# Gate products as three float32r passes, with the pieces and sums spread over ScalarE, VectorE and GpSimd

## The chip, the cores and the metric

The kernel runs on one core of a Trainium2 chip. The core has TensorE (PE in the profile, its weight loads PEld), VectorE (DVE), ScalarE (ACT), GpSimd (POOL) and SyncE (SP), which work on their own instruction streams and wait for each other through semaphores. TensorE writes its results into PSUM, which has eight banks of 128 x 512 float32. The metric is the device time of one execution in microseconds (us); the median of the runs is what is compared.

## What is computed

Sixty-four graphs of 256 nodes with 256 features pass through two residual layers with a layer norm behind each. The first is three steps of a gated graph network with shared gate weights, the second is one graph attention layer.

```python
# layer 0: x = layernorm(x + ggnn(x))
A = (adj != 0).astype(x.dtype); h = x
for i in range(3):
    m = einsum('bnd,de->bne', h, weight[i])
    aggr = einsum('bst,bsd->btd', A, m)
    gi = aggr @ w_ih.T + b_ih;  gh = h @ w_hh.T + b_hh        # 256 -> 768 each
    r = sigmoid(i_r + h_r);  z = sigmoid(i_z + h_z)
    n = tanh(i_n + r * h_n)
    h = (1 - z) * n + z * h
# layer 1: x = layernorm(x + gat(x))
Wh = x @ W;  s1 = Wh @ a1;  s2 = Wh @ a2
e = leaky_relu(s1[:, :, None] + s2[:, None, :], 0.2)
attn = softmax(where(adj > 0, e, -9e15), axis=2)
x = layernorm(x + attn @ Wh)
```

## The kernel before

Two graphs are handled together, so there are 32 pairs. A pair's hidden state lies transposed (`hT`: 2 x 128 features by 512 nodes), so that a gate is a matmul with a 128x128 weight block held and 512 columns streamed.

At the start the weights are transposed on TensorE (L120, L128) and each layer's `weight[i]` is multiplied into `w_ih` (L140, `wc`), so that the aggregation can come first: it sums `h` over the neighbours, and the gates take the result `ag` through `wc`.

For each pair `pair(p)` then does the following.

- It compares the adjacency with zero, once as a float32r matrix `A` (L245) and once as a byte mask (L247), both on VectorE, asks for the next pair's `x` and `adj`, and transposes `x` (L161).
- It runs three layers. `split` cuts `h` into a float32r part `hi` (ScalarE, L181) and the rest `lo` (VectorE, L182). `aggregate` multiplies both with the 0/1 matrix `A` as float32r (L194) and copies the sums out as `ag`. `gates` runs for each of the two feature blocks `e` (a "gate step"): four products on full float32 (L204), for the hidden part of n, for r, for the input part of n, and for z, in that order, twelve 128x128 blocks in all; then sigmoid for r (L212), `(hn + bh) * r + n_p` (L215, L216), tanh (L217), sigmoid for z (L220), `hT - n` on GpSimd (L222), times `z` (L223) and plus `n` (L224) on VectorE. After the two steps `from_T` transposes `hT` back (L170): into the next `split`, or, after the last layer, into the residual sum `v` (L265) and a layer norm.
- It does the attention layer: the transposes of `y` (L161), `wh` with both score columns (L280), the scores' transposes (L290), sums (L292), the leaky step (L294), masking (L296, L297), the maximum (L299), exponentials (L302), transposes (L312), the weighted sum (L321, L325) and a second layer norm.

A layer norm has its statistics on VectorE (L232, L234), the power -0.5 on GpSimd (L235, L236), and its application on VectorE (L238).

`pair` is a generator with 15 steps, and two pairs are active at a time, half a run apart:

```python
steps = 4 + 3 * L + 2
while started < NP or active:
    if started < NP and (not active or (len(active) == 1 and active[0][1] >= steps // 2)):
```

That gives the order in which the instructions are written. When the program is built, the framework orders each engine's stream again: it keeps to the written order where work is ready and pulls later work ahead where it isn't, as far as tile buffers are free. On the chip each stream is fixed, and an instruction that waits holds up those behind it. Four PSUM banks serve the transposes and aggregations (`ps_t`), four the gate products (`ps_g`); most work tiles have two buffers, `x` three, `adj` two, `hT` four. Copies out of PSUM that go through `evacuate` alternate between ScalarE (L73) and VectorE (L75).

## Time and profile before

| what | us |
|---|---|
| median of three runs | 2670.46 |
| the three runs | 2670.56, 2670.46, 2669.83 |
| the profiled run | 2668.64 |
| its span, first to last instruction | 2666.5 |
| TensorE busy in it | 2611.9 |
| VectorE, ScalarE, GpSimd busy | 1281.4, 829.6, 356.8 |

The granted TensorE clock of the profiled run was 0.996 of full speed. The page gives busy times of each engine, then the chain of work that ended last, then groups of instructions: line, engine, operation, the tile written and the tiles read, shape, count, then the busy time, the mean duration of one in ns, and the idle time of the engine just before them with what ended it. In the timeline a line has the start, the duration until the last of its instructions ends, the engine, the line of the kernel and the count. Matmuls overlap in their pipeline, so their pace is read from the distance of their starts and not from their duration. One float32 product shows as two matmul instructions.

### The profile page before, as it was taken

What the parts mean: (1) busy time and instruction counts of PE and PEld (TensorE: products, weight loads), DVE (VectorE), ACT (ScalarE), POOL (GpSimd) and SP (SyncE); (2) the same over time, 40 slices, a digit from 0 to 9 for tenths busy, and PEclk for the clock granted to TensorE, in tenths of its full rate; (3) what the DMA queues carried; (4) which work ended last, traced back from release to release, by engine and by line L of the source; (5) the groups of instructions that cost most, each with busy time, mean ns of one, the idle gap of its engine ahead of it and who ended that gap; (6) DMA issues with size and microseconds to landing.
All of it is one profiled execution on the core that took longest, in us unless ns stands there. A gap on an engine that the chain in (4) does not pass through costs nothing.

```text
span 2666.5 us, 23882 instructions
## 1 busy us (share of the span) xinstructions
PE 2611.9 (98%) x8928; PEld 1441.2 (54%) x8928; DVE 1281.4 (48%) x2639; ACT 829.6 (31%) x1485; POOL 356.8 (13%) x362
## 2 busy tenths in 40 slices
PE   7999999999999999999999999999999999999996
PEld 4555555555555555555555555555555555555554
DVE  2354454545445454454554545454454544545544
ACT  2233332333323333232333323333233332333332
POOL 1111111111111111111111111111111111111111
PEclk9999999999999999999999999999999999999998
DMA  3000000000000000000000000000000000000000
GB/s 95 9 16 24 16 24 16 24 16 19 22 16 24 16 24 16 16 24 18 23 24 16 24 16 24 16 16 24 16 24 16 24 16 16 24 16 16 8 0 16
DMA packets 53522, 54.48 MB, mean 20 GB/s; under 512 B 1696, under 2 KB 53408, under 8 KB 53408
## 3 DMA queue, kind: packets, MB, share of 16 engines
q1 hardware_dynamic: 52256, 51.91, 6.1%
q8 instruction: 70, 1.15, 0.2%
q10 hardware_dynamic: 1056, 1.05, 0.1%
q14 instruction: 44, 0.36, 0.0%
q0 software_dynamic: 96, 0.01, 0.0%
HBM read 36.18 MB, written 16.78 MB: 20 GB/s over the span
## 4 chain that ended last, share of the span: by engine, by line
PE 92%; DVE 4%; ACT 1%; POOL 1%; issue 1%; DMA 0%; SPq 0%; POOLq 0%; DVEq 0%; ACTq 0%
PE pg L204 73%; PE pa L194 7%; PE pwh L280 4%; PE pt L170 3%; PE po L321 2%; PE pt L161 2%; PE pt L312 1%; DVE v L325 1%; ACT z L220 1%; DVE st_b L232 1%; PE pw L140 1%; DVE o L238 1%; POOL rs_b L236 1%; PE s L290 1%; DVE d L223 1%
## 5 line engine op out<-in xcount | busy, mean ns | idle before, releaser
L204 PE MATMUL pg<-ag,wc 128*128 128x512 f32 x2304 | 1051.4, 592 | 0.0
L204 PEld LDWEIGHTS pg<-ag,wc 128*128 128x128 f32 x2304 | 437.9, 190 | 550.8 <-issue 542.2
L204 PE MATMUL pg<-hT,whhT 128*128 128x512 f32 x1536 | 719.5, 592 | 0.0
L204 PEld LDWEIGHTS pg<-hT,whhT 128*128 128x128 f32 x1536 | 276.4, 190 | 261.5 <-issue 260.6
L223 DVE TENSOR_TENSOR d<-d,z 128x512 f32<-128x512 f32 x192 | 132.8, 692 | 526.7 <-ACT z L220 500.5
L212 ACT ACTIVATE r<-pg,b_sum 128x512 f32<-128x512 f32 x192 | 131.9, 687 | 785.6 <-PE pg L204 785.4
L215 DVE SCALAR_TENSOR_TENSOR n<-pg,bh,r 128x512 f32<-128x512 f32 x192 | 144.0, 750 | 443.6 <-ACT r L212 443.6
L204 PE MATMUL pg<-xT,whhT 128*128 128x512 f32 x768 | 350.6, 592 | 0.0
L222 POOL TENSOR_TENSOR d<-hT,n 128x512 f32<-128x512 f32 x128 | 161.8, 1264 | 968.3 <-ACT n L217 968.3
L217 ACT ACTIVATE n<-n,bi 128x512 f32<-128x512 f32 x192 | 138.3, 720 | 300.7 <-DVE n L216 298.9
L220 ACT ACTIVATE z<-pg,b_sum 128x512 f32<-128x512 f32 x192 | 131.9, 687 | 315.6 <-PE pg L204 313.6
L204 PEld LDWEIGHTS pg<-xT,whhT 128*128 128x128 f32 x768 | 141.2, 190 | 153.5 <-issue 145.4
L222 POOL TENSOR_TENSOR d<-xT,n 128x512 f32<-128x512 f32 x64 | 80.9, 1264 | 513.6 <-ACT n L217 513.6
L216 DVE TENSOR_TENSOR n<-n,pg 128x512 f32<-128x512 f32 x192 | 132.1, 688 | 32.3 <-PE pg L204 25.5
L194 PE MATMUL pa<-A,lo_h 128*128 128x256 f32 x512 | 131.9, 299 | 12.2 <-DVE lo_h L182 12.1
L194 PE MATMUL pa<-A,hi_h 128*128 128x256 f32 x512 | 139.7, 309 | 0.0
L224 DVE TENSOR_TENSOR hT<-d,n 128x512 f32<-128x512 f32 x192 | 132.3, 689 | 5.5
L280 PE MATMUL pwh<-gw,yT 128*128 128x258 f32 x512 | 125.9, 388 | 0.6 <-ACT yT L73 0.5
L321 PE MATMUL po<-wh,eT 128*128 128x256 f32 x512 | 119.1, 381 | 0.0
L194 PEld LDWEIGHTS pa<-A,lo_h 128*128 128x128 f32 x512 | 95.8, 190 | 39.5 <-DVE lo_h L182 38.6
L280 PEld LDWEIGHTS pwh<-gw,yT 128*128 128x128 f32 x512 | 95.8, 192 | 38.2 <-issue 14.6
L170 PE MATMUL pt<-ident,hT 128*128 128x128 f32 x768 | 108.7, 274 | 2.9 <-DVE hT L224 2.9
(90 smaller groups left out, 2188.7 us busy)
## 6 DMA issues: line engine op xcount, KB each, us to landing
x<-in_x_dram SPq DMA_DIRECT2D x32, 512.0 KB, 3.8
adj<-in_adj_dram SPq DMA_DIRECT2D x32, 512.0 KB, 3.8
out_dram<-o SPq DMA_DIRECT2D x32, 512.0 KB, 2.9
w_n<-in_L_gnn_weight_dram ACTq DMA_DIRECT2D x1, 768.0 KB, 9.4
wi_n<-in_L_gnn_w_ih_dram SPq DMA_DIRECT2D x1, 768.0 KB, 7.0
wh_n<-in_L_gnn_w_hh_dram SPq DMA_DIRECT2D x1, 768.0 KB, 11.2
gw<-in_L_gnn_W_dram ACTq DMA_DIRECT2D x1, 256.0 KB, 10.4
bi<-in_L_gnn_b_ih_dram POOLq DMA_DIRECT2D x1, 3.0 KB, 8.0
```

What stands on the lines that cost most here:

```text
L170: nc.tensor.transpose(pt[:, (c * C + d) * P:(c * C + d + 1) * P], hT[:, d, (g * C + c) * P:(g * C + c + 1) * P], ident)
L194: nc.tensor.matmul(pt[:, g * N:(g + 1) * N], t[:, g, s, d * P:(d + 1) * P], A[:, g, s, :], start=(n == 0), stop=(n == len(todo) - 1))
L204: nc.tensor.matmul(pt, w[:, d, o * P:(o + 1) * P], m[:, d, :], start=(n == 0), stop=(n == len(todo) - 1))
L215: nc.vector.scalar_tensor_tensor(n, hn, bh[:, 2 * C + e:2 * C + e + 1], r, op0=ALU.add, op1=ALU.mult)
L216: nc.vector.tensor_add(n, n, n_p)
L217: nc.scalar.activation(n, n, AF.Tanh, bias=bi[:, 2 * C + e:2 * C + e + 1])
L220: nc.scalar.activation(z, z_p, AF.Sigmoid, bias=b_sum[:, C + e:C + e + 1])
L222: nc.gpsimd.tensor_sub(d, hT[:, e, :], n)
L223: nc.vector.tensor_mul(d, d, z)
L224: nc.vector.tensor_add(hT_new[:, e, :], d, n)
L280: nc.tensor.matmul(pt[:, :D + 2], yT[:, d, k * P:(k + 1) * P], gw[:, d, :], start=(d == 0), stop=(d == C - 1))
L321: nc.tensor.matmul(pt[:, c * D:(c + 1) * D], eT[:, g, j, c * P:(c + 1) * P], wh[:, g, j, :], start=(j == 0), stop=(j == C - 1))
```

## The change

The gate weights and both inputs of the gate products (`ag` and the hidden state) are kept as three float32r pieces each: H, the upper 12 bits; L, the rest; and D = H - L / U with U = 2^-12 (for the weights L is held scaled by 1 / U, and D is H - L). A gate product becomes two PSUM sums: the first of H x H and L x L, the second of D x D, and the result is `(1 + U) * first - U * second`. A gate step thus has 36 float32r matmuls of 512 columns in eight sums where it had 24 float32 instructions in four, and the order of the four products is now r, hidden n, z, input n.

ScalarE reads each first sum out of PSUM with the factor; VectorE subtracts the second sum from PSUM; the sigmoids then read SBUF. `r * hn`, the sum before tanh, `hT - n` and the product with `z` run on GpSimd, and the last add on VectorE; `hT` is updated in place. The pieces of `ag` are made by ScalarE (H), VectorE (L) and VectorE (D); those of the hidden state by ScalarE, GpSimd and VectorE. The adjacency comparisons and the lower half of `x` move to GpSimd, the application of the layer norm to ScalarE. In the attention layer the leaky step becomes part of the ScalarE operation (Prelu), and the mask is written over the scores in place.

PSUM is divided three to five banks; `x` has two buffers, `adj` one, `hi` and `lo` one, `hT` two, and the tiles of the attention layer one (`y` two). The core of the diff, cut:

```diff
-    io = ctx.enter_context(tc.tile_pool(name="io", bufs=3))
+    io = ctx.enter_context(tc.tile_pool(name="io", bufs=2))
-    ps_t = ctx.enter_context(tc.tile_pool(name="ps_t", bufs=4, space=bass.MemoryType.PSUM))
-    ps_g = ctx.enter_context(tc.tile_pool(name="ps_g", bufs=4, space=bass.MemoryType.PSUM))
+    ps_t = ctx.enter_context(tc.tile_pool(name="ps_t", bufs=3, space=bass.MemoryType.PSUM))
+    ps_g = ctx.enter_context(tc.tile_pool(name="ps_g", bufs=5, space=bass.MemoryType.PSUM))
...
+    def upper(dst, src):
+        nc.scalar.activation(dst, src, AF.Copy, scale=1.0 - 2.0 ** -13)
+    def lower(eng, dst, src, hi):
+        eng.tensor_sub(dst, src, hi.bitcast(F32))
+    def cross(dst, hi, lo):
+        nc.vector.scalar_tensor_tensor(dst, lo.bitcast(F32), -1.0 / U, hi.bitcast(F32),
+                                       op0=ALU.mult, op1=ALU.add)
+    def cut_weight(dst, src, tmp):
+        upper(dst[0], src)
+        lower(nc.vector, tmp, src, dst[0])
+        nc.vector.tensor_scalar(dst[1], tmp, 1.0 / U, None, op0=ALU.mult)
+        nc.vector.tensor_sub(dst[2], dst[0].bitcast(F32), dst[1].bitcast(F32))
...
+    def cut_T(hT, name):
+        cut = pieces(work, [P, C, GN], name, "h")
+        upper(flat(cut[0]), flat(hT))
+        lower(nc.gpsimd, flat(cut[1]), flat(hT), flat(cut[0]))
+        cross(flat(cut[2]), flat(cut[0]), flat(cut[1]))
+        return cut
...
-            evacuate(ag[:, d, :], pt)
+            upper(ag[0][:, d, :], pt)
+            lower(nc.vector, ag[1][:, d, :], pt, ag[0][:, d, :])
+        cross(flat(ag[2]), flat(ag[0]), flat(ag[1]))
...
-        hid, inp = (whhT, hT), (wc[:, i], ag)
-        hn = product(2 * C + e, [hid])
-        r_p = product(e, [hid, inp])
-        nc.scalar.activation(r, r_p, AF.Sigmoid, bias=b_sum[:, e:e + 1])
-        n_p = product(2 * C + e, [inp])
-        nc.vector.scalar_tensor_tensor(n, hn, bh[:, 2 * C + e:2 * C + e + 1], r, op0=ALU.add, op1=ALU.mult)
-        nc.vector.tensor_add(n, n, n_p)
+            for kinds in ((0, 1), (2,)):
+                pt = ps_g.tile([P, GN], F32, tag="g", name=f"pg_{name}_{o}")
+                todo = [(w[k], m[k], d) for k in kinds for w, m in parts for d in range(C)]
...
+        def less(dst, b, rest):
+            nc.vector.scalar_tensor_tensor(dst, b, -U, rest, op0=ALU.mult, op1=ALU.add)
+        hid, inp = (whh, hc), (wc[i], ag)
+        a, b = product(e, [hid, inp])
+        nc.scalar.activation(r, a, AF.Copy, scale=1.0 + U)
+        less(r, b, r)
+        nc.scalar.activation(r, r, AF.Sigmoid, bias=b_sum[:, e:e + 1])
+        a, b = product(2 * C + e, [hid])
+        nc.scalar.activation(n, a, AF.Identity, scale=1.0 + U, bias=bh[:, 2 * C + e:2 * C + e + 1])
+        less(n, b, n)
+        nc.gpsimd.tensor_mul(n, n, r)
+        a, b = product(C + e, [hid, inp])
+        nc.scalar.activation(z, a, AF.Copy, scale=1.0 + U)
+        less(z, b, z)
+        nc.scalar.activation(z, z, AF.Sigmoid, bias=b_sum[:, C + e:C + e + 1])
+        a, b = product(2 * C + e, [inp])
+        nc.scalar.activation(t, a, AF.Copy, scale=1.0 + U)
+        less(t, b, t)
+        nc.gpsimd.tensor_add(n, n, t)
         nc.scalar.activation(n, n, AF.Tanh, bias=bi[:, 2 * C + e:2 * C + e + 1])
-        z_p = product(C + e, [hid, inp])
-        nc.scalar.activation(z, z_p, AF.Sigmoid, bias=b_sum[:, C + e:C + e + 1])
+        d = temp("t")
         nc.gpsimd.tensor_sub(d, hT[:, e, :], n)
-        nc.vector.tensor_mul(d, d, z)
-        nc.vector.tensor_add(hT_new[:, e, :], d, n)
+        nc.gpsimd.tensor_mul(d, d, z)
+        nc.vector.tensor_add(hT[:, e, :], d, n)
...
-            nc.vector.tensor_scalar(dst[:, k // C, k % C, :], v[:, k // C, k % C, :],
-                                    mv[:, k, 0:1], rs[:, k:k + 1], op0=ALU.subtract, op1=ALU.mult)
+            nc.scalar.activation(dst[:, k // C, k % C, :], v[:, k // C, k % C, :], AF.Identity,
+                                 scale=rs[:, k:k + 1], bias=nm[:, k:k + 1])
...
-        nc.vector.tensor_scalar(A, a_sb, 0.0, None, op0=ALU.not_equal)
+        nc.gpsimd.tensor_scalar(A, a_sb, 0.0, 0.0, op0=ALU.is_equal, op1=ALU.is_equal)
-        nc.vector.tensor_scalar(mask, a_sb.rearrange("p g c n -> p (g c) n"), 0.0, None, op0=ALU.is_gt)
+        nc.gpsimd.tensor_scalar(mask, a_sb.rearrange("p g c n -> p (g c) n"), 0.0, None, op0=ALU.is_le)
...
-        hi, lo, _ = split([(g, x_sb[:, g].rearrange("p c d -> p (c d)")) for g in range(G)], f"x_{p}")
+        nc.scalar.copy(whole[1], whole[0])
+        lower(nc.gpsimd, whole[2], whole[0], whole[1])
+        hc = cut_T(hT, f"x_{p}")
...
-                                 bias=s1[:, k:k + 1])
-        nc.vector.scalar_tensor_tensor(sc, sc, ALPHA, sc, op0=ALU.mult, op1=ALU.max)
-        nc.gpsimd.memset(em, NEG_INF)
-        nc.vector.copy_predicated(em, mask, sc)
+            nc.scalar.activation(sc[:, k, :], s2r[:, (k // C) * N:(k // C + 1) * N], AF.Prelu,
+                                 bias=s1[:, k:k + 1], alpha=ALPHA)
+        nc.vector.copy_predicated(sc.rearrange("p k n -> p (k n)"), mask.rearrange("p k n -> p (k n)"),
+                                  neg.to_broadcast([P, K * N]))
```

## The prediction

> **What bounds the kernel now.** I read the page's busy shares first, then the chain that ended last, then the groups.
>
> ```profile
> PE 2611.9 (98%) x8928; PEld 1441.2 (54%) x8928; DVE 1281.4 (48%) x2639; ACT 829.6 (31%) x1485; POOL 356.8 (13%) x362
> ...
> PE 92%; DVE 4%; ACT 1%; POOL 1%; issue 1%; DMA 0%; SPq 0%; POOLq 0%; DVEq 0%; ACTq 0%
> ...
> L222 POOL TENSOR_TENSOR d<-hT,n 128x512 f32<-128x512 f32 x128 | 161.8, 1264 | 968.3 <-ACT n L217 968.3
> L217 ACT ACTIVATE n<-n,bi 128x512 f32<-128x512 f32 x192 | 138.3, 720 | 300.7 <-DVE n L216 298.9
> ```
>
> TensorE is the bound and the other engines have room; the chain's line list puts 73% of the span on the gate matmuls (L204). A 128x512 operation costs 1.264 us on GpSimd and about 0.7 us on the others. The windows view gives the steady period, two pairs long, and the drain at the end; the timeline shows how the same product runs in both.
>
> ```profile
> 1310.92:1473.05 162.13, 161.10 (x553) 88.78 (x553) 79.54 (x166) 51.37 (x92) 22.09 (x22) 1.00 0.06 20
> ...
> 2630.00:2666.50 36.50, 15.12 (x58) 11.47 (x56) 16.51 (x46) 6.84 (x17) 2.52 (x4) 0.70 0.04 14
> ```
>
> ```profile
> 1355.24 3.65 PE L280 MATMUL pwh<-gw,yT 128*128 128x258 f32 x16
> ```
>
> ```profile
> 2637.60 5.52 PE pwh L280 x16
> ```
>
> The columns after the length are busy times of PE, PEld, DVE, ACT, POOL, then the granted clock. One pair takes 162.13 / 2 = 81.07 us; 32 pairs are 2594 us, so 72 us of the 2666.5 us span are start and drain. In the drain, where PE stands idle for about 5 us at a time (2630.3 to 2635.2), the clock falls to 0.70 and `pwh` takes 5.52 us for 3.65. Last, the timeline at the boundary between two GRU layers:
>
> ```profile
> 1383.49 3.62 PE L321 MATMUL po<-wh,eT 128*128 128x256 f32 x16
> ...
> 1383.69 0.69 ACT L220 ACTIVATE z<-pg,b_sum 128x512 f32<-128x512 f32 x1 [1.93 <-PE pg L204]
> 1384.48 0.69 DVE L223 TENSOR_TENSOR d<-d,z 128x512 f32<-128x512 f32 x1 [3.53 <-ACT z L220]
> 1385.20 0.69 DVE L224 TENSOR_TENSOR hT<-d,n 128x512 f32<-128x512 f32 x1
> ...
> 1386.94 1.04 PE L170 MATMUL pt<-ident,hT 128*128 128x128 f32 x8
> ...
> 1390.53 1.38 DVE L238 TENSOR_SCALAR o<-v,mv_b,rs_b 128x256 f32<-128x256 f32 x4 [0.90 <-POOL rs_b L236]
> ...
> 1391.83 0.69 DVE L182 TENSOR_TENSOR lo_h<-pt,hi_h 128x512 fp32r<-128x512 f32 x1
> ...
> 1394.23 0.59 PE L204 MATMUL pg<-ag,wc 128*128 128x512 f32 x1
> ```
>
> From the last gate product (1383.49) to the next layer's first product on the new `ag` (1394.23) are 10.74 us, and PE idles only 0.8 us of it: it does the other pair's `po`, the transposes, the aggregation, and hidden-state products pulled ahead. This cover is what the change uses up. The view also shows blocking: the second `lo_h` waits behind `o`, which waits for GpSimd.
>
> **The products.** A gate step has 12 weight blocks. Now each is two f32 instructions: eight of them start at 1322.77 and the next at 1326.20, so 0.429 us each, 24 x 0.429 = 10.29 us. Then it is 36 float32r instructions of 512 columns, a form that the trace lacks. Bounds: half an f32 instruction, if that is two passes, 0.2145 us; or twice the 256-column float32r step of L194 (16 starts from 1308.97 about 0.119 us apart), 0.237 us. So 7.72 to 8.55 us. I take the lower, of the same width; the upper keeps a cost per weight load that is paid once, not twice, at 512 columns. Six steps a pair save 6 x 2.57 = 15.4 us (upper end 10.4). The PE floor is 81.07 - 15.4 = 65.7 us per pair.
>
> **The other engines**, over the whole run. DVE loses L215, L216, L223, half the `ag` copies, `lo_x`, both adjacency comparisons, the layer-norm applications and the leaky step (144 + 132 + 133 + 65 + 41 + 44 + 88 + 39 = 686 us), and gains 768 combinations from PSUM at 0.750 (L215), 192 subtractions at 0.66 (L182) and 192 full-width combinations at 1.226 (L294): 576 + 127 + 235 = 938. So 1281 + 252 = 1533, 48 us per pair. ACT gains 768 PSUM reads at 0.587 to 0.687 (the `ag` copy, the sigmoid), 96 more for `ag`, 96 upper halves of 1024 elements at about 1.1, 256 layer-norm applications at 0.49 (L302): some 490 + 66 + 106 + 125, so 1617, 51 us per pair. GpSimd gains 576 gate operations at 1.264, 128 subtractions of 1024 elements at about 2.5, and two adjacency comparisons a pair (nearest rows: the 1024-element fill at 0.953, twice L222 at 2.53), and loses the fill: 357 + 728 + 320 + 110 - 30 = 1485, 46 us per pair. None reaches 65.7: PE remains the bound on load alone.
>
> **The gate's tail.** After the last product came sigmoid, multiply, add: 2.4 us to 1385.89. Now there follow the subtraction of the second sum (0.75), a GpSimd add (1.264), tanh (0.72), GpSimd subtract and multiply (2 x 1.264), DVE add (0.69): 5.95 us, six hand-overs at 0.08 us (tanh's end to L222's start), and about 0.3 us until ScalarE has read the first sum, whose last matmul ends 0.43 us earlier. That is 6.7 us, 4.3 more. Between two steps of a layer this is hidden, since the next step's products need nothing of it. At a layer boundary it is not: 10.74 + 4.3 = 15.0 us, or 16.1 if the hidden state's upper half (1.1) stands on ScalarE ahead of `hi`. The lower half and the difference piece run beside the transposes and the aggregation, so I take nothing for them (0.6 us if late). PE has in it of this pair the transposes 0.87, the aggregation 16 x 0.119 = 1.9, and at most 16 hidden products at 0.2145 = 3.4 (five PSUM banks): 6.2 us. There remain 8.8 to 9.9 us. The other pair's attention and input transposes are 0.87 + 3.5 + 0.4 + 0.87 + 3.45 + 0.87 = 10 us a pair, 5 for each of the two inner boundaries (the third lies under the next pair's layer 0). So 3.8 to 4.9 us stay open, 7.6 to 9.8 us a pair, unless the next pair's first layer is pulled in; the trace shows pulls (its `pa` at 1331.11 lies ahead of the older pair's remaining L170). Between 0 and 9.8 I take 6: pulled work needs a free `x` buffer, and the blocking at 1391.83 says that queues add to it. A period of 71.7 us.
>
> **Waits.** ScalarE's tanh now waits for GpSimd, and so do its layer-norm applications (for `rs`); behind them stand the other pair's PSUM reads. DVE's `hT` add waits for GpSimd too; behind it stand the other pair's combinations and `lower`. Five banks of eight sums let PE run about 5 us ahead, which covers such a wait (the first rival is where it doesn't). With two `x` buffers the load of p+1 waits on the SP queue for pair p-1's residual add, and with one `adj` buffer for pair p's GpSimd comparisons; outputs can stand behind it. Landing takes 3.8 us, most of a pair's time lies between, DMA share is 0.06: nothing, or 3.8 us a pair if that cover is gone. The leaner softmax (no leaky step, no fill) shortens a chain that lies beside the other pair's products: nothing. Whether Prelu costs a third table load (1.283 us, now two a pair) no row shows; ACT has room.
>
> **Start and drain.** Cutting the weights puts three DVE operations and one ACT operation where 16 copies were; the matmuls wait on them: 10 to 20 us, I take 15. The last pair has no cover for three tails: 13 us.
>
> Sum: 32 x 71.7 + 72 + 28 = 2394 us span; the profiled run had 2.1 us around it (2668.64) and lies 1.8 us under the median: about 2398, and I say 2395.
>
> **A shared port.** No GpSimd subtraction overlaps a DVE operation with two SBUF inputs in this trace, which therefore can't show what overlap does. [...] By rows alone: the DVE side is 6 adds at 0.69, 6 combinations at 1.226 and the predicated copy at 1.305, 12.8 us a pair; free overlap costs nothing, and full exclusion makes 46 + 12.8 = 59 us, still under 65.7, but can put one more 1.264 us on each of two hand-overs per boundary: 5 us a pair, 2555 us. I keep zero in the sum and this end in the range.
>
> **Rivals.** (1) Slower: in-order queues bind the gate step. If each step's combinations stand behind the previous step's `hT` add, and evacuations behind sigmoid and tanh, the step is a ring: 4 x 0.75 + 3 x 0.72 + 2 x 0.69 + 3 x 1.264 + 0.69 = 11.0 us with 13 hand-overs at 0.08, 12.1 us, against 10.29 now. Six of them and twice the 8.3 us that now lie between `hT` and the `ag` products are 89 us: 32 x 89 + 104 = 2952 us. It decides once the period passes (2666 - 100) / 32 = 80.2 us, that is with half of the steps bound so. For it: the wait at 1390.53. Against: hidden products are pulled ahead of blocked work, and in the timeline most gate steps stand beside attention work, not beside another pair's gate step. (2) All gaps filled: 65.7 us, 32 x 65.7 + 104 = 2206 us. (3) The products at 0.237 us, or the port in full: 76.7 us, 2558 us. (4) Nothing pulled ahead, and the gaps cool the clock: the drain's 5 us gap made `pwh` and the transposes some 2.5 us longer; 65.7 + 9.8 + 5 = 80.5 us, 2680 us, no gain.
>
> **How the numbers follow.** Forecast 0.50, rival 2 0.15, rival 3 0.15, rival 4 0.07, rival 1 0.13. Over 0.2% (5 us, about what can be told from no change) faster: 0.83; within: 0.02; slower: 0.15. The range reaches from rival 2 past rival 3 and leaves out rivals 4 and 1, 0.20: 2200 to 2640.
>
> **What would show it.** Right: gate matmuls 0.215 us apart, a two-pair period near 143 us, PE idle some 3 us ahead of each inner aggregation, its matmuls waiting on `hi` or `lo`, and a clock of 1.00. Wrong: starts 0.237 us apart; PE waiting within a gate step on ACT or DVE for a free bank; a clock under 0.95 in the steady part; `hT` waiting long on `d` with GpSimd idle.

## The result, and the profile after

The changed kernel takes 3245.6 us (median of four, 3244.0 to 3246.5) against 2670.5 us before: 1.215 times as long, 95% interval 1.213 to 1.218. The forecast was 2395 us and faster. First the page's busy shares, utilisation of TensorE over 40 slices, and granted clock (9 is 90% or more):

```profile
PE 2666.3 (82%) x11232; PEld 2082.6 (64%) x11232; DVE 1598.8 (49%) x2807; ACT 1540.2 (48%) x2677; POOL 1594.9 (49%) x1099
...
PE   6878888888888888878888888888888888888886
...
PEclk9988888898888888888889898888889888888887
```

The three helper engines carry about what the prediction gave them (50, 48 and 50 us a pair; forecast 48, 51, 46). None is near its limit, and yet TensorE, 98% busy before, is at 82%, and many of its slices are at a clock under 0.9. So load isn't the answer; waiting is. The windows view over two pairs gives the period, 198.2 / 2 = 99 us a pair (81 before, 71.7 forecast), with the clock at 0.86:

```profile
1303.00:1501.20 198.20, 165.41 (x698) 129.59 (x697) 98.50 (x173) 95.70 (x168) 99.66 (x69) 0.86 0.05 17
```

The groups that the gate step's chain runs through (busy time, mean ns of one, then the idle time ahead of them and what ended it):

```profile
L268 POOL TENSOR_TENSOR n<-n,r 128x512 f32<-128x512 f32 x192 | 246.9, 1286 | 674.5 <-ACT r L264 573.6
L281 DVE TENSOR_TENSOR hT<-t,n 128x512 f32<-128x512 f32 x192 | 227.2, 1184 | 465.9 <-POOL t L280 465.9
...
L277 ACT ACTIVATE n<-n,bi 128x512 f32<-128x512 f32 x192 | 138.4, 721 | 231.2 <-POOL n L276 231.2
```

GpSimd stands 674 us at the multiplication by `r`; while it stands, everything behind it in its queue stands too. VectorE stands 466 us at the `hT` addition for GpSimd, and the addition itself takes 1.184 us on average, for 0.69 before. TensorE's own waits, by what ended them (us in total, times, longest; `aD` is the piece D of `ag`, `lo_h` the rest of the next layer's `h`):

```profile
PE pt L209 <- DVE hT L281: 193.3, 64, 7.2
PE pg L248 <- DVE aD L97: 81.0, 32, 4.0
PE pt L379 <- ACT sc L369: 42.5, 33, 6.3
PE pg L248 <- DVE r L257: 32.6, 16, 2.1
PE pa L233 <- DVE lo_h L94: 28.0, 15, 2.0
```

Three places in the timeline show how these waits come about.

**The tail at a layer boundary**, which the prediction drew for the old kernel between 1383.49 and 1394.23:

```profile
1681.12 1.76 DVE L281 TENSOR_TENSOR hT<-t,n 128x512 f32<-128x512 f32 x1 [1.48 <-POOL t L280]
1681.75 3.62 PE L388 MATMUL po<-wh,eT 128*128 128x256 f32 x16
...
1682.80 0.68 DVE L257 SCALAR_TENSOR_TENSOR z<-pg,z 128x512 f32<-128x512 f32 x1
1683.51 0.72 ACT L272 ACTIVATE z<-z,b_sum 128x512 f32<-128x512 f32 x1 [3.30 <-DVE z L257]
1684.14 0.58 ACT L274 ACTIVATE t<-pg 128x512 f32<-128x512 f32 x1
1684.75 0.69 DVE L257 SCALAR_TENSOR_TENSOR t<-pg,t 128x512 f32<-128x512 f32 x1 [1.27 <-ACT t L274]
...
1685.59 1.27 POOL L276 TENSOR_TENSOR n<-n,t 128x512 f32<-128x512 f32 x1 [3.26 <-DVE t L257]
...
1690.33 0.69 DVE L281 TENSOR_TENSOR hT<-t,n 128x512 f32<-128x512 f32 x1 [2.86 <-POOL t L280]
...
1691.07 1.54 PE L209 MATMUL pt<-ident,hT 128*128 128x128 f32 x6 [4.46 <-DVE hT L281]
...
1696.74 0.39 PE L233 MATMUL pa<-A,lo_h 128*128 128x256 f32 x1 [1.87 <-DVE lo_h L94]
...
1699.79 0.63 PE L248 MATMUL pg<-aH,wc2H_wc 128*128 128x512 f32 x1
```

The last gate product ends where `po` begins, 1681.75; `hT` is done at 1691.02. That is 9.3 us, 2.6 more than the forecast 6.7: the combination of `z` stood behind the previous block's `hT` addition (1681.12, stretched to 1.76), the reading of the next sum behind z's sigmoid, and so on. The whole boundary is 18.0 us (10.74 before, 15.0 to 16.1 forecast), TensorE idles 0.8 + 4.46 + 1.87 = 7.1 us of it, and the clock is half for 6.6 us of the time from 1691 to 1701.

**A tiny operation that blocks two queues:**

```profile
1594.05 3.72 POOL L304 TENSOR_SCALAR A<-adj 128x1024 fp32r<-128x1024 int32 x1 [1.05 <-PE pa L233]
...
1597.74 2.37 POOL L94 TENSOR_TENSOR lo_x<-x,hi_x 128x1024 fp32r<-128x1024 f32 x1
...
1601.46 0.16 DVE L295 SCALAR_TENSOR_TENSOR nmr_b<-mv_b,rs_b 128x4 f32<-128x4 f32 x1 [4.44 <-POOL rs_b L293]
1601.54 1.22 DVE L97 SCALAR_TENSOR_TENSOR aD<-aL,aH 128x1024 fp32r<-128x1024 f32 x1
1601.66 2.07 ACT L297 ACTIVATE y<-y,nmr_b,rs_b 128x256 f32<-128x256 f32 x4 [4.96 <-DVE nmr_b L295]
...
1602.82 1.22 PE L248 MATMUL pg<-aD,wc2D_wc 128*128 128x512 f32 x2 [4.04 <-DVE aD L97]
```

`aL` was ready at 1597.0. But on VectorE the 0.16 us `nmr_b` of the other pair's layer norm stood ahead of `aD`, waiting for `rs_b`, which on GpSimd lay behind the adjacency comparison and `lo_x`. TensorE lost 4.04 us to a chain that has nothing to do with the product. Then, in two windows, before and after this gap (busy PE, PEld, DVE, ACT, POOL, and the clock):

```profile
1594.40:1598.40 4.00, 4.00 (x18) 3.09 (x18) 2.62 (x8) 1.71 (x3) 4.00 (x2) 1.00 0.01 4
...
1603.00:1608.50 5.50, 5.50 (x13) 4.33 (x14) 1.74 (x3) 2.71 (x6) 1.27 (x1) 0.50 0.29 97
```

At a clock of 0.50 the matmuls follow each other at 0.427 us instead of 0.234: the gap was paid for twice.

**An addition beside a GpSimd subtraction:**

```profile
1515.85 2.38 POOL L94 TENSOR_TENSOR hL_x<-hT,hH_x 128x1024 fp32r<-128x1024 f32 x1
1515.92 2.85 DVE L281 TENSOR_TENSOR hT<-t,n 128x512 f32<-128x512 f32 x1 [4.37 <-POOL t L280]
1518.70 0.68 DVE L257 SCALAR_TENSOR_TENSOR r<-pg,r 128x512 f32<-128x512 f32 x1
...
1519.42 0.74 PE L248 MATMUL pg<-aH,wc2H_wc 128*128 128x512 f32 x2 [2.03 <-DVE r L257]
```

The addition of 0.69 us lasts 2.85, from just behind the start of GpSimd's subtraction to 0.5 us after its end; the combination behind it is late, and TensorE waits 2.03 us for the bank. Of the 192 `hT` additions of the run 61 are stretched like this: 31 beside this subtraction (2.83 us on average), 15 beside the multiplication by `r` (1.76) and 15 beside the mask's comparison (1.52); the median is 0.693.

**A ledger of TensorE's time.** I give each shape of matmul its 20th percentile of start-to-start times as its pace at full clock, and multiply by its count (work); add up the idle times in front of TensorE's instructions (idle); and call what remains of the stretch from its first to its last instruction the rest. Before: work 2584, idle 46, rest 20 us. After: 2206, 566, 447. The rest holds what the half clock cost, but not only that. Half of the time that TensorE was busy while the granted clock was 0.50 is an estimate of that cost: 344 us after, 4 before. What remains, about 100 and 16 us, lies at full clock, in starts further apart than the 20th percentile; why, no run says. The texts written before the runs call the whole rest half clock, which is too much. The passes did save 377 us of TensorE's work. Idle time took back 520, and the rest 427, of it 340 by the half clock.

### The profile page after: what moved, and what is told of

Its sections match the earlier page's. It is cut to its first block, busy times and chain, and to the rows that moved or that the text cites. A ratio compares the mean times of both kernels' runs of the same rounds, so it can differ in the third digit from the quotient of the medians.

```text
span 3241.9 us, 31208 instructions
## 1 busy us (share of the span) xinstructions
PE 2666.3 (82%) x11232; PEld 2082.6 (64%) x11232; DVE 1598.8 (49%) x2807; ACT 1540.2 (48%) x2677; POOL 1594.9 (49%) x1099
## 3 DMA queue, kind: packets, MB, share of 16 engines
q10 hardware_dynamic: 1056, 1.05, 0.1%
## 5 line engine op out<-in xcount | busy, mean ns | idle before, releaser
L268 POOL TENSOR_TENSOR n<-n,r 128x512 f32<-128x512 f32 x192 | 246.9, 1286 | 674.5 <-ACT r L264 573.6
L281 DVE TENSOR_TENSOR hT<-t,n 128x512 f32<-128x512 f32 x192 | 227.2, 1184 | 465.9 <-POOL t L280 465.9
L276 POOL TENSOR_TENSOR n<-n,t 128x512 f32<-128x512 f32 x192 | 246.3, 1283 | 423.6 <-DVE t L257 422.5
L209 PE MATMUL pt<-ident,hT 128*128 128x128 f32 x768 | 180.7, 363 | 248.5 <-DVE hT L281 193.3
L279 POOL TENSOR_TENSOR t<-hT,n 128x512 f32<-128x512 f32 x192 | 246.2, 1282 | 163.7 <-ACT n L277 163.7
L248 PE MATMUL pg<-hH_h,whhH_whh 128*128 128x512 f32 x768 | 292.4, 457 | 0.0
L248 PE MATMUL pg<-hD_h,whhD_whh 128*128 128x512 f32 x768 | 265.0, 424 | 2.8 <-DVE hD_h L97 1.0
L248 PE MATMUL pg<-hL_h,whhL_whh 128*128 128x512 f32 x768 | 257.1, 406 | 0.0
L280 POOL TENSOR_TENSOR t<-t,z 128x512 f32<-128x512 f32 x192 | 246.2, 1282 | 15.1
L94 POOL TENSOR_TENSOR hL_h<-hT,hH_h 128x1024 fp32r<-128x1024 f32 x64 | 151.9, 2373 | 125.3 <-ACT hH_h L91 125.3
L349 PE MATMUL pwh<-gw,yT 128*128 128x258 f32 x512 | 166.0, 464 | 25.1 <-ACT wh L79 20.1
L248 PEld LDWEIGHTS pg<-hD_h,whhD_whh 128*128 128x128 f32 x768 | 150.0, 199 | 39.6 <-DVE hD_h L97 8.0
```

The lines of the kernel that those rows point to most:

```text
L94: eng.tensor_sub(dst, src, hi.bitcast(F32))
L209: nc.tensor.transpose(pt[:, (c * C + d) * P:(c * C + d + 1) * P], hT[:, d, (g * C + c) * P:(g * C + c + 1) * P], ident)
L248: nc.tensor.matmul(pt, w[:, d, o * P:(o + 1) * P], m[:, d, :], start=(n == 0), stop=(n == len(todo) - 1))
L268: nc.gpsimd.tensor_mul(n, n, r)
L276: nc.gpsimd.tensor_add(n, n, t)
L279: nc.gpsimd.tensor_sub(d, hT[:, e, :], n)
```

## The experiments

Three theories stood at first. (1) Late chains: the gate's tail and what hangs on it make TensorE wait, and the waits cool the clock. (2) The denser float32r passes pull the clock down by themselves. (3) GpSimd's and VectorE's new loads, and a port that I took the two to share (an addition of 0.69 us lasts 2.85 beside a GpSimd subtraction at 1515.92; the port itself no run shows). For each run the table gives the time, the ratio to the kernel before, and the ledger, with the estimate of what the half clock cost; the order is by time.

| kernel | us | ratio, 95% interval | work | idle | rest | of it half clock |
|---|---|---|---|---|---|---|
| no_pool | 2387.1 | 0.8945 [0.893, 0.896] | 2210 | 91 | 60 | 5 |
| room | 2397.6 | 0.8978 [0.8965, 0.8992] | 2211 | 97 | 66 | 9 |
| put_back | 2407.5 | 0.9017 [0.9002, 0.9032] | 2198 | 101 | 84 | 7 |
| one_sum | 2476.6 | 0.9276 [0.926, 0.9291] | 2209 | 146 | 103 | 36 |
| order_only | 2506.2 | 0.939 [0.9363, 0.9417] | 2192 | 163 | 127 | 13 |
| after_one_sum | 2514.2 | 0.9416 [0.9389, 0.9444] | 2199 | 176 | 115 | 28 |
| (before) | 2670 | 1 | 2584 | 46 | 20 | 4 |
| ring_vec | 2705.6 | 1.0136 [1.0116, 1.0156] | 2203 | 290 | 187 | 96 |
| ring_only | 2711.6 | 1.0158 [1.0138, 1.0179] | 2192 | 296 | 199 | 84 |
| two_sums_vec | 2762.1 | 1.0349 [1.0319, 1.0379] | 2210 | 314 | 212 | 73 |
| ring_pool | 2875.5 | 1.077 [1.0748, 1.0791] | 2203 | 380 | 269 | 166 |
| low_dve | 3034.7 | 1.1366 [1.1333, 1.1399] | 2206 | 447 | 356 | 243 |
| mid_dve | 3053.8 | 1.1437 [1.1404, 1.147] | 2210 | 468 | 353 | 236 |
| cut_chain | 3077.3 | 1.1525 [1.1502, 1.1548] | 2206 | 548 | 302 | 192 |
| two_sums_hl | 3078.6 | 1.1531 [1.1507, 1.1554] | 2207 | 502 | 348 | 246 |
| z_last | 3136.8 | 1.1748 [1.1725, 1.1772] | 2200 | 518 | 396 | 259 |
| adj_dve | 3170.6 | 1.1875 [1.1851, 1.1899] | 2207 | 580 | 359 | 229 |
| (after) | 3245.6 | 1.2154 [1.2133, 1.2175] | 2206 | 566 | 447 | 344 |
| warm | 3294.9 | 1.234 [1.2305, 1.2376] | 2371 | 526 | 371 | 274 |

### one_sum: the passes alone

The kernel before, with only its products cut into passes; tiles share buffers to make room.

```diff
-            todo = [(w, m, d) for w, m in parts for d in range(C)]
+            todo = [(w[j], m[k], d) for j, k in ((0, 0), (0, 1), (1, 0)) for w, m in parts for d in range(C)]
...
+    def cut(dst, src):
+        nc.scalar.activation(dst[0], src, AF.Copy, scale=1.0 - 2.0 ** -13)
+        nc.vector.tensor_sub(dst[1], src, dst[0].bitcast(F32))
```

> The kernel before with its gate products alone made three float32r passes, all into one PSUM sum (H x H, H x L, L x H; the term L x L is left out); the pieces come from ScalarE and VectorE, the gate's tail, the adjacency and the layer norm stay as they were. Theory 1 (late chains, then a cooled clock): the tail stays 2.4 us, so the cover of the boundaries holds; 36 x 0.234 = 8.4 us a step against 10.29 saves 11 us a pair, period near 70 us, about 2350 us, clock over 0.97. Theory 2 (dense float32r passes pull the granted clock down by themselves): clock near 0.87, no faster than 2600 us.

2476.6 us at a clock of 0.982, with 11232 matmuls as in the changed kernel and TensorE at 94%. Theory 2 falls: as many passes, more densely packed, keep the clock. Theory 1's 2350 us isn't reached either; 127 us are missing, with 146 us of idle time. The passes by themselves take 7% off the kernel before; with what came along, the changed kernel takes 1.31 times as long as this one (3245.6 / 2476.6).

### cut_chain, adj_dve, z_last: one suspect at a time

Cut_chain leaves the recurrence out: inner layers go on from the old state, so that nothing waits for the tail, and the result isn't the network's; adj_dve has both comparisons on VectorE; z_last takes the input-n products ahead of z's.

```diff
-        nc.vector.tensor_add(hT[:, e, :], d, n)
+        nc.vector.tensor_add(hT[:, e, :] if i == L - 1 else d, d, n)
```

> The changed kernel, but in the first two layers the new state is written into a scratch tile and the next layer goes on from the old state: the recurrence over layers is left out, every instruction is still there. Theory 1: the transposes, pieces and aggregation of the next layer no longer wait for the tail; most of the 566 us of PE's idle time and of the 447 us at half clock go; 2350 to 2550 us, clock over 0.95. Theory 2 (the clock follows the float32r work): clock stays near 0.87, over 2900 us. Theory 3 (GpSimd's and VectorE's loads and the port they share): the loads are unchanged, over 2900 us.

```diff
-        nc.gpsimd.tensor_scalar(A, a_sb, 0.0, 0.0, op0=ALU.is_equal, op1=ALU.is_equal)
+        nc.vector.tensor_scalar(A, a_sb, 0.0, None, op0=ALU.not_equal)
...
-        nc.gpsimd.tensor_scalar(mask, a_sb.rearrange(...), 0.0, None, op0=ALU.is_le)
+        nc.vector.tensor_scalar(mask, a_sb.rearrange(...), 0.0, None, op0=ALU.is_le)
```

> The changed kernel with both adjacency comparisons back on VectorE (0.69 us each there; 3.66 and 2.78 us on GpSimd in the changed kernel's trace). Theory 1: only waits behind these two go, as the 4.0 us at 1602.8 on the piece aD; with the clock 100 to 250 us, so 3000 to 3150 us. Theory 3 (GpSimd's long operations are the main cause): below 2900 us.

```diff
+        a, b = product(2 * C + e, [inp])    # with its reads, addition, tanh and subtraction
         a, b = product(C + e, [hid, inp])   # with its reads and sigmoid
-        a, b = product(2 * C + e, [inp])
```

> The changed kernel with the order of the last two products of a gate step exchanged: input n before z, as in the kernel before. Theory 1: behind the last product stand then evacuation, combination, sigmoid, GpSimd multiply and add instead of combination, add, tanh, subtract, multiply, add; 2 to 3 us less on each of two inner boundaries, and with the clock 150 to 350 us less: 2900 to 3100 us. Theories 2 and 3: loads and products are the same, so within 30 us of 3246 us.

They gain 168, 75 and 109 us, and TensorE's idle time hardly moves (548, 580, 518 for 566). All three miss the range that theory 1 gave them; adj_dve and z_last miss those of the other theories too, while cut_chain's time is what theory 3 gave (over 2900 us). In adj_dve one wait did go as expected: the longest for `aD` is 1.7 us, where behind `nmr_b` it had been 4.0. In cut_chain the wait for `hT` at the boundary is all but gone (7.9 us, once), and others have grown or come in its place:

```profile
PE pg L248 <- ACT aH L91: 99.4, 46, 3.9
PE pwh L349 <- ACT wh L79: 75.2, 31, 3.2
...
PE pg L248 <- DVE hD_x L97: 58.1, 16, 3.9
```

In the changed kernel these were 19.2, 20.1 and 0.3 us. So taking away the tail at the boundary doesn't take away the idle time. I read it so that the in-order queues are late as a whole, and whichever product comes next meets it: the first theory in a wider form than the one I had written. This is argued, not shown. The framework also orders each kernel's streams anew (VectorE's stand in another order in cut_chain than in the changed kernel), and no run separates that from the waits.

### after_one_sum: the gate section put back

```diff
-            for kinds in ((0, 1), (2,)):
-                pt = ps_g.tile(...)          # two sums, pieces H, L, D
+            pt = ps_g.tile(...)              # one sum: HH, HL, LH
...
-        nc.gpsimd.tensor_mul(n, n, r)        # and ScalarE's reads, the combinations
+        nc.vector.scalar_tensor_tensor(n, hn, bh[...], r, op0=ALU.add, op1=ALU.mult)
```

> The changed kernel with the gate section alone put back: the three passes of a gate go into one PSUM sum, and the elementwise work of a gate step is that of before (ScalarE reads two sums, VectorE combines, GpSimd only subtracts); pieces are upper and lower alone, the third pass leaves the smallest product out. The adjacency comparisons and lower halves stay on GpSimd, the layer-norm application on ScalarE, the leaner attention part too. Two-sum theory (the combinations and the ring through GpSimd in each gate step make TensorE's inputs late): 2450 to 2560 us, TensorE idle under 200 us, clock over 0.97. Spread theory (GpSimd's long comparisons and lower halves, and the layer-norm constants behind them, hold the in-order queues; the gate section is innocent): still over 2900 us, idle over 400 us. Both in part: between 2600 and 2850 us.

2514.2 us, clock 0.987: in the range of the two-sum theory. 731 of the 838 us that separate the changed kernel from put_back (further down) go with the gate section: its sums, its pieces, and its ring, that is the chain of small operations from the reading of a sum to the new `hT`. The comparisons and lower pieces on GpSimd and the layer norm on ScalarE are all still there.

### mid_dve, low_dve, warm: parts of it, and the clock

```diff
-        nc.gpsimd.tensor_mul(n, n, r)
+        nc.vector.tensor_mul(n, n, r)
...
-        nc.gpsimd.tensor_add(n, n, t)
+        nc.vector.tensor_add(n, n, t)
```

> The changed kernel with two of the four GpSimd operations of a gate step (the multiplication by r and the addition of the input product) on VectorE; 12 of 24 a pair, 8.3 us more of VectorE's time a pair for 15.2 us less of GpSimd's. Queue theory (GpSimd stands at the multiplication until r is there, 574 us in all, and holds back the row constants, lower halves and subtractions behind it): GpSimd's wait for r is gone, VectorE's wait for the layer-norm constants falls from 143 us to under 80, 2950 to 3150 us. Load theory (what counts is how much VectorE carries; it goes from 50 to 58 us a pair): no gain, 3220 to 3300 us.

```diff
-        lower(nc.gpsimd, flat(cut[1]), flat(hT), flat(cut[0]))
+        lower(nc.vector, flat(cut[1]), flat(hT), flat(cut[0]))
...
-        lower(nc.gpsimd, whole[2], whole[0], whole[1])
+        lower(nc.vector, whole[2], whole[0], whole[1])
```

> The changed kernel with the lower pieces of the hidden state and of x (128 subtractions of 1024 elements) on VectorE instead of GpSimd. Shared-port theory (a GpSimd subtraction of 2.4 us that starts with the VectorE addition of hT stretches it from 0.69 to 2.85 us): the mean of the hT addition falls from 1.18 us to under 0.80, VectorE's wait for hL vanishes, 3000 to 3150 us. If neither the port nor the length of that operation is on the path that sets the end: 3200 to 3280 us, with the mean of hT down all the same.

```diff
             pt = bank("pt")
+            for n in range(warm if g == 0 else 0):      # 24 at inner boundaries
+                nc.tensor.transpose(pt[:, n % 4 * P:(n % 4 + 1) * P], ident, ident)
```

> The changed kernel with 24 transposes of the identity put ahead of the transposes at each inner layer boundary, written to the bank that those overwrite: 64 x 24 at 0.11 us, 166 us more TensorE work, standing where TensorE waits for hT (193 us in all). Clock theory (it is the gap that sets the clock to half for some us after it): idle down by 120 us or more, half-clock loss down from 447 us to under 350, and the time no longer than 3245 us although there is more to do. If the clock doesn't follow these gaps, or other gaps open in their place: half-clock loss 400 us or more, and 3270 to 3410 us.

Mid_dve gains 192 us although VectorE carries more, as the queue theory had it. One of its steps missed: VectorE's wait for the layer-norm constants didn't fall under 80 us, it stayed at 141 (112.6 and 28.1). The gain shows elsewhere: TensorE's wait for `hT` falls from 193.3 to 98.7 us, and none of the `hT` additions is stretched any more (0.692 us on average), although the lower pieces are still GpSimd's. How much of the 192 us is the queue and how much the stretched additions, the run doesn't separate. Low_dve gains 211 us; the mean of the `hT` addition falls to 0.839 us, not under 0.80, since 30 additions are still stretched, 15 beside the multiplication by `r` and 15 beside the mask's comparison.

Warm settles the clock only in part. 165 us more work cost 49 us: idle fell by 40 us, not by 120, and the rest by 76, of it the half clock by 70. The time is in the second range. So filling gaps with useless work raised the clock here (0.866 to 0.900), but where TensorE had been waiting it now waits a little later.

### ring_pool and two_sums_hl: the gate section, part by part

Ring_pool is after_one_sum with the changed kernel's order of products and its elementwise ring:

```diff
-        nc.vector.scalar_tensor_tensor(n, hn, bh[...], r, op0=ALU.add, op1=ALU.mult)
-        nc.vector.tensor_add(n, n, n_p)
...
-        nc.vector.tensor_mul(d, d, z)
...
+        nc.scalar.activation(n, product(2 * C + e, [hid]), AF.Identity, bias=bh[...])
+        nc.gpsimd.tensor_mul(n, n, r)
...
+        nc.scalar.copy(t, product(2 * C + e, [inp]))     # after z's product
+        nc.gpsimd.tensor_add(n, n, t)
...
+        nc.gpsimd.tensor_mul(d, d, z)
```

> One PSUM sum for each gate product (the third pass without the smallest product, pieces upper and lower alone), but the elementwise ring of the changed kernel: ScalarE reads all four sums, and the multiplication by r, the addition, the subtraction and the multiplication by z are GpSimd's, 24 a pair. What is gone against the changed kernel: the second sums, their 768 combinations on VectorE and the difference pieces. If the ring through GpSimd makes TensorE late: over 2800 us, idle over 350 us. If the second sums and the difference pieces do: 2500 to 2620 us, idle under 230 us. In mid_dve half of the ring's way through GpSimd was worth 190 us, so about 2510 + 300 = 2810 us if the ring's share adds up.

Two_sums_hl is the changed kernel without the difference pieces:

```diff
-            for kinds in ((0, 1), (2,)):
+            for kinds in (((0, 0), (0, 1)), ((1, 0),)):
...
-        cross(flat(cut[2]), flat(cut[0]), flat(cut[1]))
```

> The changed kernel with two sums a gate, the same combinations and the same ring through GpSimd, but of upper and lower pieces alone: the first sum holds upper x upper and upper x lower, the second lower x upper (the smallest product is left out); the difference pieces, 192 combinations of 1024 elements at 1.22 us on VectorE and their place between a piece and the products, are gone. If the difference pieces are what is late (TensorE's waits for aD and hD, some 110 us, and the half clock after them): 2950 to 3050 us. If the combinations and the ring are: 3100 to 3230 us, with TensorE's waits moved to aL and hL.

With after_one_sum and the changed kernel these make a ladder, in this order: 2514 without any of it; 2876 with the ring; 3079 with the second sums and their 768 combinations as well; 3246 with the difference pieces. The ring costs 361 us, the second sums 203, the difference pieces 167. Ring_pool lies in the range of its first theory (over 2800 us, idle over 350: 380), 65 us over the third figure; two_sums_hl lies between its two ranges. Ring_pool's largest waits are those of the ring:

```profile
PE pt L207 <- DVE hT L260: 198.1, 95, 6.4
...
DVE hT L260 <- POOL t L259: 687.0, 177, 12.7
```

### ring_vec, ring_only, order_only: what makes the ring dear

```diff
-        nc.gpsimd.tensor_mul(n, n, r)                    # ring_vec, in ring_pool
+        nc.vector.tensor_mul(n, n, r)                    # and so the addition of t and the multiplication by z
```

> Ring_pool with three of its four GpSimd operations a gate step (the multiplication by r, the addition, the multiplication by z) on VectorE; the order of the products and ScalarE's four reads stay. If the engine is the cause (each of the three takes 1.28 us instead of 0.69 and keeps GpSimd's queue closed while it waits): 2500 to 2580 us. If the order of the products (the input product last, tanh behind it) is the cause: 2700 us or more. By the length of the operations alone, two of them in the tail at 64 inner boundaries, 0.6 us each: 2875 - 77 = 2798 us.

2705.6 us, in the range of the order theory: the engine of three operations is worth 170 us, twice what the length of two of them in the tail would give (77). The other 191 us remain.

```diff
-        upper(flat(cut[0]), flat(hT))                    # ring_only: ring_pool's gate step in put_back
-        lower(nc.gpsimd, flat(cut[1]), flat(hT), flat(cut[0]))
+        for d in range(C):
+            upper(cut[0][:, d, :], hT[:, d, :])
+            lower(nc.vector, cut[1][:, d, :], hT[:, d, :], cut[0][:, d, :])
```

> Put_back (2407.5 us) with the GpSimd ring of ring_pool in the gate step and nothing else on GpSimd but the row constants: the comparisons and the lower pieces stay on VectorE. If the ring is slow by its own length and hand-overs: 2650 to 2780 us, about as much over put_back as ring_pool is over after_one_sum (361 us). If it is slow only because it shares GpSimd's queue with the long comparisons and lower pieces: 2420 to 2520 us.

2711.6 us, 304 over put_back. The ring is dear even when GpSimd has little else to do; sharing its queue with comparisons and lower pieces adds the rest (ring_pool is 164 over ring_only, after_one_sum 107 over put_back: 57 us more with the ring than without).

```diff
-        hn = product(2 * C + e, [hid])                   # put_back: hn, r, n_p, z
         r_p = product(e, [hid, inp])
+        hn = product(2 * C + e, [hid])
...
         z_p = product(C + e, [hid, inp])
+        n_p = product(2 * C + e, [inp])                  # order_only: r, hn, z, n_p; its addition and tanh after it
```

> Put_back (2407.5 us) with only the order of a gate step's products that the change has: r, hidden n, z, input n, so that the addition, tanh, subtraction, multiplication and hT addition all follow the last product, where put_back has only the sigmoid of z, a multiplication and an addition there. Nothing else moves. If the order carries what the engine doesn't (ring_vec stayed 191 us over after_one_sum): 2560 to 2620 us, with TensorE waiting for hT at the 64 inner boundaries. If ScalarE's two more reads carry it: 2400 to 2450 us.

2506.2 us: the order alone costs 99 us. I expected 150 to 210 if the order carried all that ring_vec left, so it carries about half. Whether ScalarE's two more reads carry the other 92, or the order is dearer in ring_vec's surroundings, or it is the buffers (in the ring `t` and the difference `hT - n` share two, in after_one_sum the difference has two for itself), stays open. TensorE's wait for `hT` in order_only is only 17.3 us (5.4 in put_back). Its idle time rises by 62 us in several places: it waits 28.0 us for a `wh` that put_back never waits for, 18.1 for `lo_h` (8.5), 22.8 for `eT` (17.5).

### two_sums_vec: can the two sums be kept?

```diff
-        nc.gpsimd.tensor_mul(n, n, r)                    # in z_last
+        nc.vector.tensor_mul(n, n, r)                    # and so the addition of t and the multiplication by z
```

> The changed kernel, its two sums and difference pieces kept, with the input-n products ahead of z's (as in z_last) and three of the four GpSimd operations of the gate step on VectorE. If engine and order in the gate step are most of the loss, the two gains add: 3245 - 108 (z_last) - 190 to 300 (mid_dve and the third operation) = 2840 to 2950 us. If they carry it nearly whole: under 2700 us, and the two sums would pay. VectorE then carries 62 us a pair.

2762.1 us: order and engine together are worth 483 us, more than I had added up (up to 409). But it falls between the two ranges and stays 3.5% over the kernel before. Its largest wait, `pg <- aD`, 71.1 us, is not one for the difference piece's own length: all 16 of these waits stand behind `nmr_b`, which waits for GpSimd's `rs_b` as at 1601.46. GpSimd still has the comparisons and lower pieces there. Put_back has them on VectorE and is 107 us under after_one_sum; whether two sums would pay with that too, no run shows.

### put_back, room, no_pool: a faster kernel

Put_back is after_one_sum with comparisons and lower pieces on VectorE; what remains of the change is the three passes, the layer norm on ScalarE and the leaner attention part. Room adds buffers:

```diff
-    io = ctx.enter_context(tc.tile_pool(name="io", bufs=2))
+    io = ctx.enter_context(tc.tile_pool(name="io", bufs=3))
...
-    # in words: ps_t 3 banks, ps_g 5 banks; late, hi, lo and adj: 1 buffer
+    # in words: ps_t 4 banks, ps_g 4 banks; late, hi, lo and adj: 2 buffers
+    # and the hidden state's pieces are made in gates(), per feature block
```

> After_one_sum with the lower pieces, by blocks of 512, and the adjacency comparisons back on VectorE; the leaner attention part and the layer-norm application on ScalarE stay. Its waits there for hL (50 us) are gone: 2440 to 2480 us, idle under 140 us, against 2477 us for one_sum; if VectorE's larger load (36 to 44 us a pair) matters more: 2500 to 2540 us.

> Put_back with more buffers (three for x, two for adj, for the pieces of h and for the tiles of the attention part), four banks for either kind of PSUM tile instead of three and five, and the hidden state's pieces cut as soon as each feature block is done: 2420 to 2460 us and a clock over 0.985 if waits for free tiles hold the attention part; 2450 to 2480 us if they do not.

No_pool takes the last gate operation off GpSimd:

```diff
-        nc.gpsimd.tensor_sub(d, hT[:, e, :], n)
+        nc.vector.tensor_sub(d, hT[:, e, :], n)
```

> Room (2397.6 us) with the last GpSimd operation of the gate step, the subtraction h - n, on VectorE as well: the tail is 0.6 us shorter, VectorE carries 4 us a pair more. 2380 to 2395 us if the tail is still on the path at the layer boundaries (64 x 0.6 = 38 us at most), 2395 to 2405 us if it is hidden.

2407.5, 2397.6 and 2387.1 us; the last is 10.6% under the kernel before. Put_back and room are faster than I expected, no_pool is in its first range. Room's buffers, banks and earlier pieces together bring 10 us. Put_back is 69 us under one_sum, so what is left of the change (the leaner attention part, the layer norm on ScalarE, its division of buffers) does help once the gate step isn't in its way; these parts were not run one by one. The timeline at a layer boundary of no_pool, to be held against that of the changed kernel above:

```profile
1210.97 0.63 PE L242 MATMUL pg<-aH,wc0L_wc 128*128 128x512 f32 x2
1211.44 3.65 PE L334 MATMUL pwh<-gw,yT 128*128 128x258 f32 x16
1211.64 0.69 ACT L258 ACTIVATE z<-pg,b_sum 128x512 f32<-128x512 f32 x1 [1.19 <-PE pg L242]
1212.36 0.69 DVE L261 TENSOR_TENSOR d<-d,z 128x512 f32<-128x512 f32 x1 [1.18 <-ACT z L258]
...
1213.24 0.68 DVE L262 TENSOR_TENSOR hT<-d,n 128x512 f32<-128x512 f32 x1
...
1214.93 1.03 PE L207 MATMUL pt<-ident,hT 128*128 128x128 f32 x8
...
1220.38 0.64 PE L242 MATMUL pg<-aH,wc1H_wc 128*128 128x512 f32 x2
```

From the last product (1211.44) to `hT` 2.5 us, to the first product on the new sums 8.9; TensorE's idle time in it is 0.06 us.

## Why the prediction was wrong

The sum missed by 848 us of span (3241.9 against 2394). By the ledger: TensorE's work fell by 377 us instead of 493, 116 us; idle time rose by 520 us instead of the 220 that the sum held (6 us a pair, and 28 for start and drain), 300 us; the rest rose by 427 instead of nothing, of it 340 by the half clock. That is 843 of the 848.

- **Products at 0.2145 us**: mis-sized. They follow each other at 0.234 us (two in 0.47 us, from 1680.82 to 1681.29), close to the upper bound of 0.237 that I had put aside with the argument that a weight load is paid once; what the 0.234 us are made of, no run shows. A step is 36 x 0.234 = 8.4 us; the mechanism, fewer passes, was right, and one_sum shows what it brings.
- **Other engines' load**: right, and useless. That none reaches TensorE's 66 us a pair says nothing on whether its results come in time.
- **The gate's tail**: the rows were added up as if each operation started when its input was there. 6.7 us forecast, 9.3 in the boundary shown, because each of the engines had something else in front. The inner boundary is 18.0 us for 15.0 to 16.1.
- **6 us of idle a pair at the boundaries**: this is the step that failed. I counted work of the other pair as cover for this pair's tail. But the other pair's work needs the same three queues, and can stand behind the same waits: 16.4 us a pair, (198.20 - 165.41) / 2. Cut_chain shows that it isn't a sum over boundaries: without the wait there, 548 us of idle time are left. After_one_sum shows where it comes from: with the gate section alone put back, 176.
- **Waits "covered by five banks"**: wrong. 4.44 us at `nmr_b`, 4.96 at `y`; five banks hold two and a half products of two sums each, where four banks had held four products. I had quoted such a block from the old profile (`lo_h` at 1391.83, behind `o`), and then gave it no price of its own, only a part in choosing 6 between 0 and 9.8.
- **Difference pieces and lower halves beside other work, "nothing"**: 167 us for the former (two_sums_hl), 211 us for the latter on GpSimd, with those of `x` (low_dve).
- **No clock cost in the sum**: the largest single miss, some 340 us. I had it as a rival (80.5 us a pair, 5 of them for the clock) at a chance of 0.07. Over the runs of the table the half clock grows with the idle time, but faster than it: 0.05 to 0.25 us for each us of idle in the kernels with 91 to 176 us of it, 0.23 to 0.61 in those with 290 us or more.
- **The adjacency comparisons on GpSimd**, estimated at 0.953 to 2.53 us: 3.687 and 2.788. On VectorE (adj_dve) they take 0.748 and 0.684. Moving them was worth 75 us.
- **The shared port at zero**: wrong; a price of zero doesn't fit the rows. That the two engines share a port and that one shuts the other out was an assumption of mine: no run shows a port, nor the full exclusion that the 2555 us and rival 3 count with. What the rows show is that an addition can last longer beside a GpSimd operation. At 1515.92 one takes 2.85 us for 0.69: 2.31 us of it lie beside a GpSimd operation that had started 0.07 us earlier, and 0.54 behind that one's end. Beside the mask's comparison the addition ends 1.2 us ahead of it, so there it doesn't last as long as the other operation. The mean of the `hT` addition, 1.184 us in the changed kernel, is 0.687 in put_back. The bound that I gave, 5 us a pair, took it as 1.264 us on two hand-overs of each boundary; how much of low_dve's 211 us is this stretching and how much GpSimd's queue, no run separates.
- **Start and drain**: +28 us forecast; 3241.9 - 32 x 99.1 = 71 us, where the kernel before has 72. My sum was also uneven: the forecast adds 100 us for start and drain (72 + 28), the rivals 104.
- **x and adj buffers at nothing**: room, with more of them and of other things, gains 10 us over put_back; in the changed kernel no run tried it.
- **Rival 1**, in-order queues that bind the gate step, 89 us a pair and 2952 us: the right kind, at a chance of 0.13. It was short of the half clock, and it priced a ring that must turn in 12.1 us, not other work standing behind the ring. What I held against it, that steps stand beside attention work and not beside another gate step, was no protection: at 1601.46 it is the other pair's layer norm that stands in the way.
- **What would show it wrong**: starts 0.234 us apart (0.237 named), TensorE waiting within a gate step (`pg <- r`, 32.6 us), a clock under 0.95, `hT` waiting long on GpSimd's product (466 us): these came. GpSimd wasn't idle meanwhile, as that sign had it; it was at work in 404 of the 466 us.

## What to carry to other kernels

When small operations are spread over engines to even out loads, count hand-overs and head-of-queue waits, not busy time: take each engine's instructions in their order, and ask what stands behind each wait, the other stream's work above all. In this kernel it paid to put the products whose results have the longest way to go first (99 us in order_only), to sum in PSUM as long as the arithmetic allows (203 us), and to keep a chain that crosses GpSimd off the path between two matmuls (304 us in ring_only). And price TensorE's idle time at more than itself: with the half clock on the work behind it, a us of it cost 1.05 to 1.25 us in the kernels here that have little, 1.23 to 1.61 in those that have much.

## What the runs showed of the hardware

The granted clock in the traces of the kernel before and of the changed kernel is 1.0 or 0.5, in pieces of 3.4 us or a multiple, and in the changed kernel a gap shorter than such a piece can be enough: behind the 1.87 us at 1696.74 the next piece was at half.

```profile
1694.30:1697.70 3.40, 1.53 (x13) 1.33 (x12) 1.78 (x3) 1.58 (x4) 1.50 (x3) 1.00 0.00 0
1697.70:1701.10 3.40, 3.40 (x12) 2.72 (x11) 2.47 (x4) 2.39 (x5) 2.94 (x1) 0.50 0.45 154
```

TensorE was busy for 1.53 of the first 3.40 us, 45%, and the following 3.40, in which it never stood, ran at 0.50. The changed kernel as a whole, in pieces of 3.4 us, says the same: behind a piece at 1.0 in which TensorE was busy for less than half, the next was at 0.50 in 113 of 114 cases; behind one busy for 70% or more, in none of 521. From 0.50 the clock came back behind 127 of the 135 pieces that were busy for 80% or more, and behind none of the 119 others.

In the changed kernel the clock fell 128 times, and the half clock cost, by the estimate of the ledger, 344 of its 3242 us, 11%.
